# Seeding a PSUM bank with D u, and a planner that dates the parts of a ScalarE block

## The chip, the cores and the metric

The kernel runs on one core of one Trainium2 chip. The metric is the device time of the program in microseconds, median of several runs. All data is float32.

## The reference, cut to what matters

The program is a two-layer network on 8 images of 384 channels x 32 x 32. Layer 0 is a selective state-space block (mamba) in both directions over the 1024 positions plus a gated local convolution. Layer 1 is causal attention with six heads, and a feed-forward part with quantised activations for the first five images. What the change touches:

```python
def step(h, inp):
    dA, dBu, c = inp
    h = dA * h + dBu
    return (h, jnp.einsum('bdn,bn->bd', h, c))
...
y = ys.transpose(1, 0, 2) + u * D_param
y = y * silu(z)
...
h = _bitlinear(x, W1, b1)
h = jax.nn.gelu(h, approximate=False)
out = _bitlinear(h, W2, b2)
```

The states' sum over n, the term D u and the gate silu(z) are the first part of the change. `_bitlinear` scales its result by 128 over the largest magnitude and clips it, and the gelu's input is clipped only where it matters (from above, after the gelu); the second product reads those clips.

## The kernel before

**The scan.** The work of the state-space block is cut into 768 units. A unit is one image, one direction and half of the positions (a "part", four per image), one of three blocks of 128 channels, one of four groups of four states, and one of two halves `q` of the channel block; each unit is a tile g of 128 partitions x 1024. For a unit, GpSimd multiplies delta u by B into g (`s_first`, line 988), ScalarE forms exp(delta A) in a PSUM bank `da`, VectorE scans along the positions, ScalarE copies the last column as a carry in parts that have a successor, and GpSimd multiplies g by C (`s_scan`, line 994). There are six g buffers, and GpSimd's first multiply runs two units ahead. Two units make a pair: TensorE sums the four states of the pair into the single PSUM bank `y` (`s_sum`, line 1020), with the matmul's start flag at the first of four pairs and its stop flag at the last. After eight units the part of that channel block closes (`s_gate`, line 1040): u is loaded from DRAM (one buffer), and VectorE forms D u + y into an SBUF tile `yt` for the direction that comes first. For the second it forms D u + y in the bank, adds `yt`, and multiplies by the gate `z`, and the product goes to DRAM. So 48 closings take one VectorE instruction and 48 take three, and only then may TensorE begin the next sums in the same bank.

**Beside it** run, from lists of steps, the input projections and convolutions of the next images, attention, and the feed-forward part. Its middle (lines 1419 to 1427) is one block of four gelus of 128 x 3072 on ScalarE and a table load, recorded with `together()` so that nothing comes between them, followed by four VectorE clips. The 12 products of each of six groups (line 1432 on) read the four clipped quarters in turn. ScalarE reads each finished group out of its bank. The input gates record a similar block of silus and tanhs.

**The order** is made by a planner. Every instruction is recorded first as an `Op` (line 152); several instructions recorded together are the parts of one `Op`. `record` (line 189) adds up a modelled cost for it and notes in `before` which earlier ops it must follow, by overlapping boxes of the tiles. `place` (line 246) then goes through modelled time: an op becomes ready when the modelled ends of its predecessors are past (plus a signal time of 0.2 when they are on another engine), and each free engine takes the ready op of lowest rank. The rank is the order of recording, less what `hurry` grants: 600 for the scan's slots, 60 for gates, clips and blocks. The resulting order is emitted engine by engine, and each engine's queue then runs in that order on the chip, waiting on semaphores. A block's end in the model is the end of all of its parts, its last table load included.

Of the kernel before, what the change touches and what calls it, by code (L numbers as in the profile page):

```python
# [10 lines left out]
F32 = mybir.dt.float32  # L11
BF16 = mybir.dt.bfloat16
AF = mybir.ActivationFunctionType
ALU = mybir.AluOpType
# [4 lines left out]
P = 128  # L19
# [3 lines left out]
HB = 512  # L23
# [31 lines left out]
V_NORM, V_CW, V_CB, V_DTB, V_D, V_DW, V_DWB, V_BP, V_B2 = 0, 1, 5, 6, 7, 8, 17, 18, 19  # L55
# [3 lines left out]
class View:  # L59


    def __init__(self, tile, ap):
        self.tile, self.ap = tile, ap
# [88 lines left out]
class Op:  # L152
    def __init__(self, name, what, args, kwargs, rank):
        self.name, self.parts, self.rank = name, [(what, args, kwargs)], rank
        self.before, self.behind, self.left = {}, [], 0
        self.tiles = []
        self.ready, self.start, self.end = 0.0, None, None
        self.time = 0.0


class Plan:
# [15 lines left out]
    @contextmanager  # L177
    def together(self):
        self.group = []
        yield  # L180
        self.group = None

    @contextmanager
    def hurry(self, offset):
        self.sooner += offset
        yield
        self.sooner -= offset

    def record(self, name, what, args, kwargs):
        views = [v for v in list(args) + list(kwargs.values()) if isinstance(v, View)]  # L190
        given = kwargs.get("out", args[0] if args else None)
        written = [v for v in (given, kwargs.get("accum_out")) if isinstance(v, View)]
        if self.group:
            op = self.group[0]
            op.parts.append((what, args, kwargs))
        else:
            op = Op(name, what, args, kwargs, len(self.ops) - self.sooner)
            self.ops.append(op)
            if self.group is not None:
                self.group.append(op)  # L200
        cost = self.cost(name, what, args, kwargs, written, views)
        if name == "tensor":
            op.time = max(op.time, cost)
        else:
            op.time += cost
        for v in views:
            t, box = v.tile, v.box()
            write = any(v is w for w in written)
            if not t.users:
                t.order = len(t.kind.queue)  # L210
                t.kind.queue.append(t)
            for other, b in t.writes + (t.reads if write else []):
                if other is not op and not (b[1] < box[0] or box[1] < b[0] or b[3] < box[2] or box[3] < b[2]):
                    op.before[id(other)] = other
            (t.writes if write else t.reads).append((op, box))
            if not t.users or t.users[-1] is not op:
                t.users.append(op)
            if t not in op.tiles:
                op.tiles.append(t)
# [26 lines left out]
    def place(self):  # L246
# [7 lines left out]
        def names(op):  # L254
            return ("scalar", "vector") if op.name == "any" else (op.name,)

        def release(op):
            op.ready = max(
                [b.end + (0.0 if b.name == op.name and not b.dma else self.SIGNAL) for b in op.before.values()],
                default=0.0,  # L260
            )
            for e in names(op):
                heapq.heappush(waiting[e], (op.ready, next(count), op))
                heapq.heappush(events, (op.ready, next(count), e))

        for op in self.ops:
            op.dma = op.parts[0][0] == "dma_start"
            op.left = len(op.before)
            for b in op.before.values():
                b.behind.append(op)  # L270
        users_left = {id(t): len(t.users) for k in self.kinds.values() for t in k.queue}
        for op in self.ops:
            if not op.left:
                release(op)
# [19 lines left out]
        while events:  # L294
# [4 lines left out]
            while moved:  # L299
                moved = False  # L300
                for e in engines:
                    while waiting[e] and waiting[e][0][0] <= now:
                        op = heapq.heappop(waiting[e])[2]
# [5 lines left out]
                    while free_at[e] <= now and ready[e]:  # L309
                        aside, op, held = [], None, set()  # L310
                        while ready[e]:
# [3 lines left out]
                            if fits(item[2], now, held):  # L315
                                op = item[2]
# [7 lines left out]
                        for t in op.tiles:  # L324
                            if t.place is None:
                                k = t.kind
# [10 lines left out]
                        for t in op.tiles:  # L337
                            users_left[id(t)] -= 1
                            if not users_left[id(t)]:
                                at = max(u.end for u in t.users) + self.SIGNAL  # L340
# [10 lines left out]
    def real(self, v, place):  # L351
        if not isinstance(v, View):
            return v
        home = v.tile.kind.places[place]
        return bass.AP(home.tensor, v.ap.offset, v.ap.ap)
# [25 lines left out]
def kernel(  # L381
# [21 lines left out]
    nc = plan = Plan(tc, homes)  # L403
    together, hurry = plan.together, plan.hurry
# [5 lines left out]
    sp = Pool(plan, "scan", 2, bass.MemoryType.SB)  # L410
# [3 lines left out]
    def ctile(name, shape, dt=F32):  # L414
        return const.tile(shape, dt, name=name, tag=name)
# [12 lines left out]
    def bank(name, tag=None):  # L428
        tag = tag if tag in BANKS else "any"
        return ps.tile([P, HB], F32, name=name, tag=tag, bufs=BANKS[tag])  # L430
# [4 lines left out]
    def half(h):  # L435
        return slice(h * HB, (h + 1) * HB)
# [4 lines left out]
    def load(dst, src):  # L441
        nc.sync.dma_start(out=dst, in_=src)
# [8 lines left out]
    spilled = {}  # L451
# [8 lines left out]
    vec = ctile("vec", [P, NC, NV])  # L460
# [8 lines left out]
    for d in range(2):  # L469
        nc.scalar.dma_start(out=wdt[d * DW : d * DW + RANK, :], in_=w_dt)  # L470
        nc.scalar.dma_start(
            out=wdt[d * DW + RANK : d * DW + RANK + 1, :],
# [10 lines left out]
    wproj = ctile("wproj", [P, NC, C])  # L483
    nc.scalar.dma_start(out=wproj, in_=w_proj.rearrange("(c p) e -> p c e", p=P))

    ident = ctile("ident", [P, P])
    make_identity(tc.nc, plan.now(ident))

    cmask = ctile("cmask", [P, HB], BF16)
    nc.vector.memset(cmask, 0.0)  # L490
# [468 lines left out]
    sst = {}  # L959
# [16 lines left out]
    def s_row(u, i):  # L976

        if u.c > 0 or u.q > 0:
            return
        r = sp.tile([P, HB], F32, name=f"bc{i}_{u.name}", tag=f"bc{i}", bufs=NG)  # L980
        rows = spilled[u.b, "rows", u.d][i * NS + u.j * SUB : i * NS + (u.j + 1) * SUB, half(u.h)]
        load(r, rows.partition_broadcast(BLK))
        sst["bc", i, u.b, u.part, u.j] = r
# [36 lines left out]
    def s_sum(u):  # L1020

        if u.q == 0:
            sst["pair"] = sst.pop(("g", u.name))
            return
        if u.j == u.first_group:
            sst["y"] = bank(f"y_{u.name}", "y")
        y = sst["y"]
        pair = (sst.pop("pair"), sst.pop(("g", u.name)))
        with together():
            for k in (2, 3, 0, 1):  # L1030
                nc.tensor.matmul(
                    out=y[k * BLK : (k + 1) * BLK, :],
                    lhsT=gather,
                    rhs=pair[k // 2][:, k % 2, :],
                    start=(u.j == u.first_group),
                    stop=(u.j == u.last_group),
                    skip_group_check=True,
                )

    def s_gate(u):  # L1040

        if not u.closes:
            return
        b, c, h, y = u.b, u.c, u.h, sst["y"]
        key = ("yt", b, c, h)
        t = sp.tile([P, HB], F32, name=f"uh_{u.name}", tag="us", bufs=1)
        load(t, spilled[b, "u", u.d, c][:, half(h)])
        if key not in sst:
            yt = sp.tile([P, HB], F32, name=f"yt_{u.name}", tag="yt", bufs=2 * NC)
            with hurry(offset=60):  # L1050
                nc.vector.scalar_tensor_tensor(
                    yt, t, vec[:, c, V_D : V_D + 1], y, ALU.mult, ALU.add
                )
            sst[key] = yt
            return
        z = sp.tile([P, HB], F32, name=f"zh_{u.name}", tag="z", bufs=1)
        load(z, spilled[b, "z", c][:, half(h)])
        yt = sst.pop(key)
        with hurry(offset=60):
            nc.vector.scalar_tensor_tensor(y, t, vec[:, c, V_D : V_D + 1], y, ALU.mult, ALU.add)  # L1060
            nc.vector.tensor_tensor(y, yt, y, ALU.add)
            nc.vector.tensor_tensor(z, z, y, ALU.mult)
        gy = dram.tile([P, HB], F32, name=f"sgy_{u.name}", tag=f"sp_gy_{c}_{h}")
        nc.sync.dma_start(out=gy, in_=z)
        spilled[b, "gy", c, h] = gy
# [440 lines left out]
    def slots(lo, hi):  # L1506
        def at(f, k):
            if 0 <= k < len(units):
                f(units[k])

        def slot(k):
            at(s_load, k + AHEAD + 2)
            at(lambda u: s_row(u, 0), k + AHEAD + 2)
            at(lambda u: s_row(u, 1), k + 2)
            at(s_first, k + AHEAD)
            at(s_scan, k)
            at(s_sum, k - 1)
            at(s_gate, k - 1)

        def ahead_of_all(k):  # L1520
            with hurry(offset=600):
                slot(k)

        return [(lambda k=k: ahead_of_all(k), 5.0) for k in range(lo, hi)]
# [62 lines left out]
    at = 0.0  # L1587
# [61 lines left out]
```

## Time and profile before

| | |
|---|---|
| median of 3 runs | 4044.43 us (4044.12 to 4044.86) |
| the profiled execution | 4048.24 us |
| its span, first to last instruction | 4046.4 us |
| TensorE clock granted, mean | 0.900 |
| GpSimd's scan multiplies, first start to last end | 74.8 to 3861.3 us |
| VectorE's D u and y steps | 48 x 740, 48 x 747 and 48 x 696 ns |
| gelu block of image 1, first start to last end | 1604.65 to 1615.75 us |

The page gives busy times by engine over the span, the same in 40 slices, and groups of instructions with what ended the idle time before them. Engines are PE (TensorE), DVE (VectorE), ACT (ScalarE), POOL (GpSimd) and SP (SyncE, which issues most DMAs). A matmul of the program in float32 is two instructions in the profile. As all instructions are issued through one recording helper, they bear the same line (L367), so groups are told apart by the names of their tiles: `scan_g` is g, `ps_y` the bank y, `ps_da` the exponentials, `scan_us` the loaded u, `big_big` and `mid_mid` the large tiles of attention and feed-forward.

### The profile page before, as it was taken

The numbers are of one execution on the slowest core, as the hardware profiler recorded it, in microseconds if no ns is written. First come the engines' busy times: TensorE is split into PE (matmuls) and PEld (weight loads), VectorE is DVE, ScalarE is ACT, GpSimd is POOL, SyncE is SP. The second block draws the span as 40 slices with busy tenths as digits, with TensorE's granted clock in tenths as the row PEclk, the third lists the DMA queues.
The fourth block names the chain that finished last, engine by engine and source line by source line (L and its number), as shares of the span: only waits on it lengthen the run. The fifth ranks groups of instructions, "written<-read, shape, count | busy, mean of one in ns | idle before, by whom it ended". The sixth has DMA issues, their size and how long they took to land. (4 is left out here: it accounts for less than half of the span.)

```text
span 4046.4 us, 42961 instructions
## 1 busy us (share of the span) xinstructions
PE 3387.3 (84%) x12426; PEld 1330.0 (33%) x12426; DVE 3264.4 (81%) x4580; ACT 2546.6 (63%) x4967; POOL 3570.8 (88%) x1559
## 2 busy tenths in 40 slices
PE   5585679888699897998986989969989699898899
PEld 1121223333134332343332333323433233333344
DVE  5888987889977899678897687996779977778843
ACT  5666665866746766547667377664676654847635
POOL 2999999999999999789998799987899997999910
PEclk8685779899799898899997999979999799999999
DMA  7547655343563344742445533446334473333300
GB/s 237 194 141 242 235 191 174 100 144 126 202 209 124 102 147 135 247 157 86 134 161 195 183 110 105 138 169 242 123 100 138 142 266 127 113 122 108 128 16 32
DMA packets 338965, 611.99 MB, mean 151 GB/s; under 512 B 34616, under 2 KB 93416, under 8 KB 338728
## 3 DMA queue, kind: packets, MB, share of 16 engines
q1 hardware_dynamic: 329072, 593.10, 43.3%
q10 hardware_dynamic: 9656, 16.15, 1.2%
q8 instruction: 98, 1.61, 0.2%
q14 instruction: 139, 1.14, 0.1%
HBM read 456.03 MB, written 153.09 MB: 151 GB/s over the span
## 5 line engine op out<-in xcount | busy, mean ns | idle before, releaser
L367 POOL TENSOR_TENSOR scan_g<-scan_ud,scan_bc 128x1024 f32<-128x1024 f32 x768 | 1815.9, 2369 | 164.7 <-PE ps_y L367 97.0
L367 POOL TENSOR_TENSOR scan_g<-scan_g,scan_bc 128x1024 f32<-128x1024 f32 x768 | 1816.6, 2369 | 120.9 <-ACT scan_carry L367 66.0
L367 ACT ACTIVATE ps_da<-scan_dl,const_amat 128x512 f32<-128x512 f32 x1536 | 1052.6, 691 | 813.7 <-DVE scan_g L367 800.6
L367 DVE TENSOR_TENSOR_SCAN scan_g<-ps_da,scan_carry,scan_g 128x512 f32<-128x512 f32 x768 | 940.0, 1267 | 111.1 <-POOL scan_g L367 88.0
L367 PE MATMUL ps_any<-big_big,mid_mid 128*128 128x512 f32 x2016 | 952.9, 625 | 78.4 <-DVE big_big L367 56.5
L367 DVE TENSOR_TENSOR_SCAN scan_g<-ps_da,scan_g 128x512 f32<-128x512 f32 x768 | 893.1, 1206 | 127.8 <-POOL scan_g L367 86.9
L367 PE MATMUL ps_y<-scan_g,const_gather 128*32 128x512 f32 x3072 | 467.8, 686 | 275.1 <-POOL scan_g L367 265.0
L367 PEld LDWEIGHTS ps_any<-big_big,mid_mid 128*128 128x128 f32 x2016 | 388.0, 199 | 662.9 <-issue 486.3
L367 PE MATMUL ps_any<-big_big,big_big 128*128 128x512 f32 (+4 forms) x1728 | 551.9, 558 | 15.9 <-DVE small_nm L367 5.3
L367 PE MATMUL ps_any<-const_ident,mid_mid 128*128 128x128 f32 x1728 | 309.4, 304 | 96.0 <-DVE small_nm L367 44.1
L367 DVE CUSTOM_DVE_ANT_0 mid_mid<-ps_any,const_cmask 128x512 f32<-128x512 f32 (+3 forms) x576 | 291.2, 546 | 70.7 <-PE ps_any L367 69.7
L367 PEld LDWEIGHTS ps_any<-big_big,big_big 64*128 64x128 f32 (+1 forms) x1728 | 223.1, 189 | 309.9 <-issue 199.0
L367 DVE SCALAR_TENSOR_TENSOR ps_any<-big_big,const_vec,ps_any 128x496 f32<-128x496 f32 (+6 forms) x420 | 303.1, 727 | 21.6 <-ACT ps_any L367 11.9
L367 PEld LDWEIGHTS ps_any<-const_ident,mid_mid 128*128 128x128 f32 x1728 | 197.9, 149 | 331.2 <-DVE small_nm L367 100.3
L367 ACT COPY ptp_ptn<-ps_any 128x512 f32<-128x512 f32 (+3 forms) x576 | 255.2, 478 | 47.3 <-PE ps_any L367 38.4
L367 PE MATMUL ps_any<-ptp_ptn,big_big 128*64 128x512 f32 (+3 forms) x1152 | 262.3, 536 | 14.6 <-ACT ptp_ptn L367 13.1
L367 ACT ACTIVATE mid_mid<-mid_mid,small_low 128x512 f32<-128x512 f32 (+3 forms) x384 | 242.3, 634 | 47.5 <-DVE small_low L367 47.5
L367 PEld LDWEIGHTS ps_y<-scan_g,const_gather 128*32 128x32 f32 x3072 | 64.2, 114 | 545.0 <-POOL scan_g L367 443.6
L367 PE MATMUL ps_any<-mid_mid,const_onesc 128*128 128x512 f32 x252 | 131.2, 655 | 60.5 <-ACT mid_mid L367 45.6
L367 ACT ACT_TABLE_LOAD x131 | 168.1, 1283 | 2.9 <-PEq L1636 0.7
L367 PE MATMUL ps_any<-mid_mid,const_wdt 25*128 25x512 f32 x192 | 132.1, 852 | 41.6 <-DVE mid_mid L367 32.2
L367 DVE COPY big_big<-ps_any 128x512 f32<-128x512 f32 (+1 forms) x86 | 54.2, 631 | 128.6 <-PE ps_any L367 128.6
(100 smaller groups left out, 3185.4 us busy)
## 6 DMA issues: line engine op xcount, KB each, us to landing
scan_dl<-dram_sp_dl SPq DMA_DIRECT2D x384, 256.0 KB, 3.3
scan_ud<-dram_sp_ud SPq DMA_DIRECT2D x384, 256.0 KB, 3.7
scan_bc<-dram_rows SPq DMA_DIRECT2D x256, 256.0 KB, 3.4
scan_us<-dram_sp_u SPq DMA_DIRECT2D x96, 256.0 KB, 2.7
mid_mid<-dram_sp_u SPq DMA_DIRECT2D x96, 256.0 KB, 4.9
dram_sp_dl<-mid_mid SPq DMA_DIRECT2D x96, 256.0 KB, 4.0
dram_sp_ud<-mid_mid SPq DMA_DIRECT2D x96, 256.0 KB, 4.6
dram_sp_u<-mid_mid SPq DMA_DIRECT2D x42, 512.0 KB, 4.9
```

The costliest lines, as they stand in the source:

```text
L367: getattr(engine, what)(*[mapped(v) for v in args], **{k: mapped(v) for k, v in kwargs.items()})
```

## The change

Part one: the u tile of a part is loaded (`s_skip`, recorded five units before it is used, two buffers), and at the part's opening ScalarE writes D u into the bank `y` (`s_seed`). For the second direction VectorE adds `yt` to it there. All sums then accumulate (`start=False`) on what the bank holds. At the closing the first direction is copied by ScalarE to `yt`, the second is multiplied by `z` by VectorE. One matmul with a start flag at the program's beginning marks the whole bank as written by TensorE.

Part two: an `Op` keeps the modelled end of each of its parts (`upto`), a predecessor is noted together with the last of its parts that matters, and readiness is taken from that part's end (`ends`) and not from the block's.

```diff
@@ class Op
-        self.time = 0.0
+        self.time, self.upto = 0.0, []
+
+    def ends(self, part):
+
+        if self.name == "tensor" or self.dma:
+            return self.end
+        return self.start + self.upto[part]
@@ def record
+        op.upto.append(op.time)
+        part = len(op.parts) - 1
...
-            for other, b in t.writes + (t.reads if write else []):
+            for other, n, b in t.writes + (t.reads if write else []):
...
-                    op.before[id(other)] = other
-            (t.writes if write else t.reads).append((op, box))
+                    op.before[id(other)] = (other, max(n, op.before.get(id(other), (None, 0))[1]))
+            (t.writes if write else t.reads).append((op, part, box))
@@ def place, release
-                [b.end + (0.0 if b.name == op.name and not b.dma else self.SIGNAL) for b in op.before.values()],
+                [
+                    b.ends(n) + (0.0 if b.name == op.name and not b.dma else self.SIGNAL)
+                    for b, n in op.before.values()
+                ],
@@ the beginning
+    nc.tensor.matmul(
+        out=bank("written", "y"),
+        lhsT=ident,
+        rhs=wproj.rearrange("p c e -> p (c e)")[:, :HB],
+        start=True,
+        stop=True,
+    )
@@ def s_sum
-        if u.j == u.first_group:
-            sst["y"] = bank(f"y_{u.name}", "y")
...
-                    start=(u.j == u.first_group),
+                    start=False,
@@ the scan's gates
+    def s_skip(u):
+
+        if not u.opens:
+            return
+        t = sp.tile([P, HB], F32, name=f"uh_{u.name}", tag="us", bufs=2)
+        load(t, spilled[u.b, "u", u.d, u.c][:, half(u.h)])
+        sst["us", u.b, u.c, u.part] = t
+
+    def s_seed(u):
+
+        if not u.opens:
+            return
+        t, y = sst.pop(("us", u.b, u.c, u.part)), bank(f"y_{u.name}", "y")
+        yt, scale = sst.pop(("yt", u.b, u.c, u.h), None), vec[:, u.c, V_D : V_D + 1]
+        with hurry(offset=60):
+            nc.scalar.activation(y, t, AF.Copy, scale=scale)
+            if yt is not None:
+                nc.vector.tensor_tensor(y, yt, y, ALU.add)
+        sst["y"], sst["second"] = y, yt is not None
...
-        t = sp.tile([P, HB], F32, name=f"uh_{u.name}", tag="us", bufs=1)
-        load(t, spilled[b, "u", u.d, c][:, half(h)])
-        if key not in sst:
+        if not sst["second"]:
             yt = sp.tile([P, HB], F32, name=f"yt_{u.name}", tag="yt", bufs=2 * NC)
             with hurry(offset=60):
-                nc.vector.scalar_tensor_tensor(
-                    yt, t, vec[:, c, V_D : V_D + 1], y, ALU.mult, ALU.add
-                )
+                nc.scalar.copy(yt, y)
...
         with hurry(offset=60):
-            nc.vector.scalar_tensor_tensor(y, t, vec[:, c, V_D : V_D + 1], y, ALU.mult, ALU.add)
-            nc.vector.tensor_tensor(y, yt, y, ALU.add)
             nc.vector.tensor_tensor(z, z, y, ALU.mult)
@@ def slot
+            at(s_skip, k + 4)
             at(s_scan, k)
+            at(s_seed, k - 1)
             at(s_sum, k - 1)
             at(s_gate, k - 1)
```

More of the change, by code (lines that the diff above doesn't have):

```diff
@@ L268, in place @@
             op.left = len(op.before)
-            for b in op.before.values():
+            for b, _ in op.before.values():
                 b.behind.append(op)
@@ L1044, in s_gate @@
         b, c, h, y = u.b, u.c, u.h, sst["y"]
-        key = ("yt", b, c, h)
-        t = sp.tile([P, HB], F32, name=f"uh_{u.name}", tag="us", bufs=1)
-        load(t, spilled[b, "u", u.d, c][:, half(h)])
-        if key not in sst:
+        if not sst["second"]:
             yt = sp.tile([P, HB], F32, name=f"yt_{u.name}", tag="yt", bufs=2 * NC)
             with hurry(offset=60):
-                nc.vector.scalar_tensor_tensor(
-                    yt, t, vec[:, c, V_D : V_D + 1], y, ALU.mult, ALU.add
-                )
-            sst[key] = yt
+                nc.scalar.copy(yt, y)
+            sst["yt", b, c, h] = yt
             return
@@ L1057, in s_gate @@
         load(z, spilled[b, "z", c][:, half(h)])
-        yt = sst.pop(key)
         with hurry(offset=60):
-            nc.vector.scalar_tensor_tensor(y, t, vec[:, c, V_D : V_D + 1], y, ALU.mult, ALU.add)
-            nc.vector.tensor_tensor(y, yt, y, ALU.add)
             nc.vector.tensor_tensor(z, z, y, ALU.mult)
```

## The prediction

> **What bounds the kernel now.** I began with the page's busy times and its 40 slices, since the kernel has several stages with different limits.
>
> ```profile
> PE 3387.3 (84%) x12426; PEld 1330.0 (33%) x12426; DVE 3264.4 (81%) x4580; ACT 2546.6 (63%) x4967; POOL 3570.8 (88%) x1559
> POOL 2999999999999999789998799987899997999910
> PEclk8685779899799898899997999979999799999999
> ```
>
> GpSimd (POOL) is the fullest engine and runs at nine tenths nearly everywhere. It holds 1536 scan multiplies that follow each other about every 2.32 us (1536 starts fill the 3562.5 us that their union covers). The dips stand a few slices apart. Windows cut around them show which stages they are:
>
> ```profile
> 1100.00:1600.00 500.00, 492.25 (x214) 0.92 0.46 154
> 1600.00:1860.00 260.00, 218.65 (x95) 0.89 0.51 174
> 1860.00:2130.00 270.00, 267.11 (x116) 0.96 0.39 129
> 2130.00:2400.00 270.00, 222.53 (x97) 0.89 0.50 169
> 2670.00:2900.00 230.00, 184.62 (x80) 0.90 0.53 182
> 3200.00:3420.00 220.00, 178.94 (x78) 0.89 0.56 193
> 3420.00:3862.00 442.00, 439.55 (x190) 0.96 0.34 112
> ```
>
> The columns are window, length, POOL busy, instructions, clock, DMA share, GB/s. In the four stages in which images 1 to 4 go through gelu and the second feed-forward product, POOL idles 41.4 + 47.5 + 45.4 + 41.1 = 175 us. All other time between its start (75 us) and its end (3861 us) has some 45 us of idle. After that come 185 us of the last image's attention, without POOL. The page's chain of waits covers only part of that tail (some 3% of the span), so it does not decide; POOL's own waits do:
>
> ```profile
> POOL scan_g L367 <- PE ps_y L367: 97.0, 24, 12.5
> POOL scan_g L367 <- ACT scan_carry L367: 66.0, 45, 8.1
> POOL scan_g L367 <- DVE scan_g L367: 42.6, 24, 10.9
> ```
>
> (Total us, times, longest.) The first line: the six g buffers are full, because TensorE has not yet summed them. Of its 97.0 us, 22.8 + 24.2 + 28.2 + 18.4 = 93.6 lie in those four stages. The other two lines are ScalarE and VectorE being late with the scan. The timeline of image 1 shows both kinds (start, duration, what, count, idle before it):
>
> ```profile
> 1604.65 11.10 ACT L367 ACTIVATE big_big<-big_big,small_qs 128x3072 f32<-128x3072 f32 x4
> 1615.77 2.57 ACT L367 ACT_TABLE_LOAD   x2
> 1618.35 2.95 ACT L367 ACTIVATE mid_mid<-mid_mid 128x1024 f32<-128x1024 f32 x3
> 1617.46 9.19 DVE L367 TENSOR_SCALAR big_big<-big_big 128x3072 f32<-128x3072 f32 x4
> 1621.69 12.31 PE L367 MATMUL ps_any<-big_big,mid_mid 128*128 128x512 f32 x24 [8.96 <-DVE big_big L367]
> 1629.69 7.14 POOL L367 TENSOR_TENSOR scan_g<-scan_g,scan_bc 128x1024 f32<-128x1024 f32 x3 [9.67 <-DVE scan_g L367]
> 1699.40 20.87 PE L367 MATMUL ps_any<-big_big,mid_mid 128*128 128x512 f32 x48
> 1721.37 4.69 POOL L367 TENSOR_TENSOR scan_g<-scan_ud,scan_bc 128x1024 f32<-128x1024 f32 x2 [7.57 <-PE ps_y L367]
> ```
>
> ScalarE's gelus and the silus right behind them hold it from 1604.65 to 1623.72, 19 us. The clips wait on VectorE for all of the gelus, the products on TensorE for the clips, and POOL starves 9.67 us. Later TensorE pays the delay back: 24 products (48 instructions) in a row, 20.87 us between two sums that POOL's pace would have 9.3 us apart, and POOL stops 7.57 us.
>
> **D u and the gates.** Removed from VectorE: 48 x 740 ns + 48 x 747 ns = 71 us (the groups scan_yt<-scan_us and ps_y<-scan_us). Added to ScalarE: 96 scaled copies into the bank, by the nearest row (ps_any<-big_big,const_vec, 685 ns) 66 us, and 48 copies of y, by ptp_ptn<-ps_any at 128x512 (584 ns), 28 us. ScalarE goes from 2547 to about 2640 us (65%), VectorE from 3264 to about 3193. POOL does none of it, so the sum on the path is nothing by itself. One matmul is added at the start; its weight lands at 10.4 + 12.7 = 23.1 us and TensorE is next wanted at 24.60, so it is nothing.
>
> What frees the y bank changes from one or three VectorE steps (0.74; 0.75 + 0.70 + 0.69 = 2.1 us) to copy and seed (0.58 + 0.69 = 1.3), or product, seed and addition (0.69 + 0.69 + 0.70 = 2.1). So as long as it is not queued, the chain is the same. The next sum is due 9.3 us later, and in the quiet stages POOL is full (492 of 500 us) with today's chain. Queued behind a waiting copy are ScalarE's exponentials of the next units, and VectorE's scans wait for those; today the same wait, 54.7 us in 30 of 96 closings, stands on VectorE, which is the fuller engine. I bound the effect by -5 and +30 us on POOL and take +5, near the row that shows no loss. The u loads (96, 2.7 us) move from the closing to five units before use with a second buffer; SyncE's queue today waits 532 us for the one buffer, yet POOL waits only some 5 us for DMAs after its start, so I count nothing. If that queue blocked the scan loads instead, it would be in those 30.
>
> **Where each engine's work now stands.** The order of instructions of both builds holds no times, but says what TensorE must do between two pairs of sums. I priced a product at 2 x 0.43 us (20.87/48) and let work queue up that exceeds the 8.3 us which POOL's 9.3 us leave beside the sums' own 1.0. The largest backlog of the stages of images 1 to 4:
> before 27.6, 30.0, 30.9, 33.1 us; after 0.6, 24.1, 20.8, 19.0 us.
> Before, POOL lost 93.6 us for 121.6 us of backlog, so about 7 us of each is absorbed by the buffers. With that, after loses 0 + 17 + 14 + 12 = 43 us: a gain of 50 us. The second image gains most: its bursts of 20.6, 18.1, 18.1 and 17.4 us become runs of 7.7.
>
> **The gelus.** Clips stand behind each gelu and no longer behind the block and some 15 convolution steps, and for images 1 to 4 the silu block now stands three or more units behind the gelu block. ScalarE is then held 11.1 + 1.3 us, not 19. The four gaps at the gelus (9.7, 10.9, 7.1, 8.1: 36 us) can shrink by 6.7 each (2.95 + 1.22 of silus and tanhs, two table loads of 1.28), 27 us at most. Two things eat into it. First the clips themselves. This is their record:
>
> ```profile
> 1617.46 4.18 DVE L367 TENSOR_SCALAR big_big<-big_big 128x3072 f32<-128x3072 f32 x1
> ...
> 1621.56 1.75 DVE L367 TENSOR_SCALAR big_big<-big_big 128x3072 f32<-128x3072 f32 x1
> ```
>
> The first one took 4.18 us although it needs 1.75: it ended 1.6 us after POOL's last multiply (1620.02). The Trainium skill, page "SBUF — State Buffer", section "Who interferes with whom", says that such an operation and GpSimd exclude each other for a whole instruction, and that whoever comes first wins. That speaks against this change: clips now fall where POOL still works. By the rule 20 clips x 1.75 = 35 us of POOL may be lost; by the row POOL's next multiply (1617.67) went ahead of a clip already waiting, and the clip ran in POOL's idle time, which costs VectorE and not POOL. I take 8 us, nearer the row. The second: ScalarE's reading of the first finished product stands one or two units behind the gelus, while the product ends some 4 us later; 2 to 3 us in each of four places, 10 us. Net gain 27 - 8 - 10 = 9 us.
>
> **Sum.** -50 - 9 + 5 = -54 us on the profiled execution's span of 4046.4. That execution took 4048.2 us, 3.8 over the median of the runs; I apply the difference to the median: 4044.4 - 54 = 3990 us.
>
> **Rivals.**
> - Everything falls into place: no burst outgrows the buffers (93.6 us) and half of the gelu gaps go (18): -112 us, 3932. For it: POOL is shown full wherever its feeders are smooth. Against it: bursts of 18 to 24 us remain in the new order. With less, down to 3965, 15%.
> - The promised order is not what the chip sees: the clips wait for POOL to starve, so the products start no sooner (TensorE comes out of a stretch at half clock either way), and the bursts wander. Only about 15 us remain: 4030. For it: the lock above. 20%, of which 6% within 0.2% of no change.
> - Slower: seeds and copies on ScalarE. ScalarE takes its work in order; if at each of the 96 part boundaries it waits for TensorE's last sum or VectorE's product with the next exponentials behind it, POOL pays p each time. With p = 1.0 us (of the 1.8 us that VectorE now waits when it waits) that is 96 instead of my 5: 4044 - 59 + 96 = 4081. It is slower than before from p = 0.6 on, and measurably from 0.7. Against it: the quiet stages, where POOL loses next to nothing to such closings on the fuller engine. 15%.
> - My forecast, 50%, 3965 to 4012.
>
> **How the numbers follow.** About 0.2% (8 us) is what a measurement of this kernel can tell from no change. Faster: 50 + 15 + 14 = 79%; same 6%; slower 15%. The range from 3945 to 4050 leaves out the better half of the first rival and most of the slower one.
>
> **What would show it.** In the changed profile POOL's wait for PE ps_y should be about 45 us, near nothing in image 1's stage; runs of TensorE products between sums there some 8 us. The gelu block should end in one table load with exponentials behind it, and POOL's gaps there should be 3 to 7 us. VectorE's busy time should fall by about 71 us, ScalarE's rise by about 90. POOL should stay near full in the stages between. I am wrong if POOL's waits for ACT scan_carry or DVE scan_g grow by as much as the first falls (the boundaries), if clips stretch POOL's multiplies beyond 2.37 us, or if the four stages still hold 170 us of idle.

## The result, and the profile after

The changed kernel takes 4002.52 us (median of 4 runs, 3999.95 to 4005.82), the kernel before in the same session 4044.27 us (4042.36 to 4044.86). The ratio is 0.9898, with a 95% interval of 0.9881 to 0.9915. So 41.8 us were gained, where 54 were forecast, and the time lies inside the range. The profiled execution of the changed kernel took 3999.95 us, its span is 3998.2. That is 48.2 us less than the span before. The difference from 41.8 is where the two profiled executions lie beside their medians, and nothing in the kernel. The sums below are made against the 48.2.

The busy times and the slices of GpSimd and of TensorE's clock, from the page of the changed kernel:

```profile
PE 3389.8 (85%) x12428; PEld 1330.5 (33%) x12428; DVE 3215.7 (80%) x4484; ACT 2629.5 (66%) x5111; POOL 3582.3 (90%) x1559
POOL 3999999999899998999999899988999889999910
PEclk8696879998899997999987999989999889999999
```

VectorE is 49 us less busy, not 71: the 20 clips, whose waiting counts as busy, took 61.4 us in all and not 42.4. ScalarE is 83 us more busy. GpSimd's dips have become shallow. Windows cut around the same stages, as far from each gelu block as those of before (window, length, POOL busy, clock, DMA share, GB/s; the first line is the quiet stretch ahead of image 1's gelu):

```profile
1043.00:1533.00 490.00, 483.18 (x210) 0.93 0.47 159
1533.00:1793.00 260.00, 243.13 (x106) 0.90 0.52 177
2073.00:2343.00 270.00, 246.32 (x105) 0.85 0.49 170
2622.00:2852.00 230.00, 199.80 (x85) 0.90 0.53 185
3150.00:3370.00 220.00, 187.91 (x80) 0.89 0.57 197
```

The four feed-forward stages now hold 16.9 + 23.7 + 30.2 + 32.1 = 103 us of idle, where they held 175. GpSimd's waits show which part went:

```profile
POOL scan_g L378 <- ACT scan_carry L378: 78.6, 32, 10.2
POOL scan_g L378 <- PE ps_y L378: 40.0, 15, 6.8
POOL scan_g L378 <- DVE scan_g L378: 36.8, 24, 4.8
```

The wait for TensorE's sums fell from 97.0 to 40.0 us. The wait behind ScalarE's carry did not fall, it rose from 66.0 to 78.6. The timeline of image 1's gelu says why (start, duration, what, count, idle before it):

```profile
1537.34 11.10 ACT L378 ACTIVATE big_big<-big_big,small_qs 128x3072 f32<-128x3072 f32 x4
1539.41 7.00 POOL L378 TENSOR_TENSOR scan_g<-scan_ud,scan_bc 128x1024 f32<-128x1024 f32 x3
1540.23 7.79 DVE L378 TENSOR_SCALAR big_big<-big_big 128x3072 f32<-128x3072 f32 x1 [0.66 <-ACT big_big L378]
1548.08 9.76 PE L378 MATMUL ps_any<-big_big,mid_mid 128*128 128x512 f32 x18 [11.26 <-DVE big_big L378]
1548.45 1.28 ACT L378 ACT_TABLE_LOAD   x1
1560.97 0.69 ACT L378 ACTIVATE big_big<-ps_any,const_vec 128x512 f32<-128x512 f32 x1 [8.73 <-PE ps_any L378]
1562.84 2.35 POOL L378 TENSOR_TENSOR scan_g<-scan_g,scan_bc 128x1024 f32<-128x1024 f32 x1 [9.53 <-ACT scan_carry L378]
```

The gelus now end in one table load, as planned. The first clip starts 2.9 us after the gelus begin, but it ends at 1548.02, 1.6 us after GpSimd's third multiply (1546.41), and needs 1.75 itself: three multiplies in a row went ahead of it. TensorE's products therefore start at 1548.08. ScalarE's reading of the first finished product, which stands one unit behind the gelus in its queue, then waits 8.73 us with the next exponentials behind it, and GpSimd starves 9.53 us. Image 0 goes the same way:

```profile
1000.66 7.78 DVE L378 TENSOR_SCALAR big_big<-big_big 128x3072 f32<-128x3072 f32 x1
1020.69 0.69 ACT L378 ACTIVATE big_big<-ps_any,const_vec 128x512 f32<-128x512 f32 x1 [8.89 <-PE ps_any L378]
1023.17 2.35 POOL L378 TENSOR_TENSOR scan_g<-scan_g,scan_bc 128x1024 f32<-128x1024 f32 x1 [10.16 <-ACT scan_carry L378]
```

In images 2 to 4 the reading stands one and a half or two units behind the gelus, and does not wait at all. In image 2 the clips came first, and GpSimd paid in another way:

```profile
2089.82 1.73 DVE L378 TENSOR_SCALAR big_big<-big_big 128x3072 f32<-128x3072 f32 x1
2090.05 3.72 POOL L378 TENSOR_TENSOR scan_g<-scan_g,scan_bc 128x1024 f32<-128x1024 f32 x1 [0.64 <-DVE scan_g L378]
```

A multiply that takes 2.35 us alone took 3.72, since a clip of 1.73 had begun 0.23 us before it.

**One account for all kernels.** A span is the time up to GpSimd's first multiply, the union of its multiplies, its idle time between them, and the tail after the last. I divide the idle time by the place where a gap ends: in the 40 us after the start of one of the five gelu blocks ("gelu"), from 40 to 240 us after it ("products"), and everywhere else ("quiet"). This is added up from the starts and ends in each trace, in us:

| kernel | start | gelu | products | quiet | union | tail | span |
|---|---|---|---|---|---|---|---|
| before | 74.8 | 51.7 | 131.5 | 40.9 | 3562.5 | 185.2 | 4046.4 |
| changed | 72.7 | 40.0 | 80.0 | 45.1 | 3574.0 | 186.4 | 3998.2 |
| e1 seeds only | 77.0 | 42.3 | 89.3 | 31.2 | 3566.4 | 183.6 | 3989.8 |
| e2 planner only | 72.3 | 51.8 | 86.3 | 61.9 | 3573.2 | 185.2 | 4030.7 |
| e3 gelu block by its end | 75.2 | 48.1 | 62.0 | 41.3 | 3566.2 | 185.2 | 3977.8 |
| e4 other form of clip | 73.5 | 59.4 | 77.0 | 41.1 | 3559.8 | 185.0 | 3995.8 |
| e5 model alone | 74.8 | 51.5 | 99.0 | 67.5 | 3565.5 | 176.1 | 4034.4 |
| e6 gelu alone | 75.2 | 47.2 | 116.6 | 32.9 | 3575.5 | 183.5 | 4030.9 |
| e7 clip dated longer | 73.8 | 39.8 | 99.9 | 39.4 | 3573.4 | 185.2 | 4011.6 |
| e8 gates later | 74.1 | 39.1 | 59.8 | 44.1 | 3572.9 | 186.5 | 3976.5 |
| e9 early u | 76.6 | 48.1 | 110.5 | 48.3 | 3566.5 | 185.2 | 4035.2 |
| e10 seeds on VectorE | 74.9 | 54.0 | 118.4 | 126.4 | 3575.4 | 180.2 | 4129.1 |
| e11 other form, dated | 74.5 | 41.3 | 97.1 | 43.4 | 3560.1 | 185.2 | 4001.6 |
| e12 nudged | 73.5 | 49.5 | 91.3 | 46.7 | 3567.2 | 183.6 | 4011.7 |

### The profile page after: what moved, and what is told of

The parts are those of the page before. It is cut to its first block, busy times and chain, and to the rows that moved or that the text cites. A ratio compares the mean times of both kernels' runs of the same rounds, so it can differ in the third digit from the quotient of the medians.

```text
span 3998.2 us, 43071 instructions
## 1 busy us (share of the span) xinstructions
PE 3389.8 (85%) x12428; PEld 1330.5 (33%) x12428; DVE 3215.7 (80%) x4484; ACT 2629.5 (66%) x5111; POOL 3582.3 (90%) x1559
## 5 line engine op out<-in xcount | busy, mean ns | idle before, releaser
L378 POOL TENSOR_TENSOR scan_g<-scan_g,scan_bc 128x1024 f32<-128x1024 f32 x768 | 1828.2, 2383 | 121.5 <-ACT scan_carry L378 78.6
L378 POOL TENSOR_TENSOR scan_g<-scan_ud,scan_bc 128x1024 f32<-128x1024 f32 x768 | 1838.9, 2398 | 103.1 <-DMA scan_ud<-dram_sp_ud 59.5
L378 PE MATMUL ps_any<-ptp_ptn,big_big 128*64 128x512 f32 (+3 forms) x1152 | 267.2, 544 | 13.4 <-ACT ptp_ptn L378 12.4
L378 ACT ACTIVATE mid_mid<-mid_mid,small_low 128x512 f32<-128x512 f32 (+3 forms) x384 | 242.5, 634 | 42.3 <-DVE small_low L378 42.0
L378 PE MATMUL ps_any<-mid_mid,const_onesc 128*128 128x512 f32 x252 | 130.2, 652 | 42.3 <-ACT mid_mid L378 30.9
L378 ACT COPY mid_mid<-ps_any 128x512 f32<-128x512 f32 x234 | 130.9, 582 | 43.0 <-PE ps_any L378 36.4
```

The source lines that it names most:

```text
L378: getattr(engine, what)(*[mapped(v) for v in args], **{k: mapped(v) for k, v in kwargs.items()})
```

## The experiments

My theory after the result: the gain is the shorter bursts of products, and dating the gelus by their parts gives back what it saves. Rivals: one of the two parts of the change does it all; or the order is chance.

**e1, the seeds alone, and e2, the planner alone.** Each keeps one part of the diff above and the other side as it was before.

> Only the first part of the change (D u seeded into the bank); the planner dates blocks by their end as before. The order of its instructions already differs: largest TensorE backlog between sums in the stages of images 1 to 4 7.7, 29.6, 24.8 and 27.6 us (before 27.6, 30.0, 30.9, 33.1). Theory (TensorE's bursts decide): POOL's wait for PE ps_y falls from 97 to about 62 us, and two of four silu blocks leave the gelus: 4005 to 4020 us. Rival (dating the parts is all of the gain, seeds are neutral): 4040 to 4048 us. Rival (ScalarE's closings cost POOL at each boundary): over 4052 us.

> Only the second part (parts of blocks dated); the gates stay as before. Backlogs in its order 2.0, 26.9, 27.4, 23.9 us. Theory (bursts decide, either part can smooth them): POOL waits about 57 us for PE ps_y, total 4002 to 4015 us. Rival (the gain is the 71 us that leave VectorE): 4035 to 4048 us.

The seeds alone took 3992.6 us (ratio 0.9872, 0.9858 to 0.9885), less than the whole change and 12 us under the range of its theory. The planner alone took 4032.9 us (0.9972, 0.9962 to 0.9983), near the range of its rival and 18 us above that of its theory. Both shorten the bursts: the idle time under the products falls by 42 and by 45 us. The planner alone pays it back, with 21 us more in the quiet stages and 11 us of stretched multiplies; the seeds alone lose nothing there, their quiet stages improve by 10.

**e3, the change with the gelu block dated by its end.** Every other block is still dated by its parts.

```diff
     def ends(self, part):
...
+        if any(k.get("func", None) == AF.Gelu or AF.Gelu in args for _, args, k in self.parts):
+            return self.end
```

> The whole change, but the gelu block alone is dated by its end as before, so clips and products stand late again, while silus, tanhs and softplus are dated part by part. Backlogs in its order 0.7, 22.4, 24.8, 20.2 us, about those of the change; silus stand right behind the gelus again for images 2 to 4. Theory (bursts decide, and early clips collide with POOL's multiplies, which eats what the gelus gain): within 10 us of the changed kernel, 3993 to 4012 us. Rival (early clips and products are the gain): 4025 to 4044 us.

It took 3977.2 us (0.9835, 0.9821 to 0.9848): 25 us better than the changed kernel and 16 us under the range of its theory. The profiled spans differ by 20 us. Of these, the changed kernel saves 8 us of gaps at the gelus, loses 8 us to stretched multiplies, 18 us more under the products, and 4 us in the quiet stages.

**e4, the clips in another form, in the changed kernel's order.** The clip is min, then an addition of 0 with an accumulator; the values are the same.

```diff
...
-    nc.vector.tensor_scalar(st["h", q], st["h", q], QCLIP, None, ALU.min)
+    nc.vector.tensor_scalar(
+        st["h", q], st["h", q], QCLIP, 0.0, ALU.min, ALU.add, accum_out=sink
+    )
```

> The changed kernel with the clip in the form that also gives a sum (min, then adding 0), in exactly the same order. The page on SBUF says this form does not take GpSimd's port. Theory (the clip and POOL's multiplies exclude each other): clips last about 3.3 us each but never stretch a multiply, which stays at 2.32 to 2.37 us, the first clip is never held 7.8 us, the 10 us gaps for ACT scan_carry at images 0 and 1 shrink to under 4; 3978 to 3992 us. Rival (the exclusion is a side show): 3998 to 4008 us. If the longer clips delay products as much as the lock did: 4000 to 4010 us too, with the gaps kept but no stretched multiply.

It took 3998.4 us (0.9888, 0.9872 to 0.9903), in the range of the first rival and not of the theory. The clips by form (min/median/max ns, first and last start), first of the changed kernel, then of e4:

```profile
L378 DVE TENSOR_SCALAR big_big<-big_big x20: 1731/2634/7790, 1000.7 to 3176.2; 128x3072 f32<-128x3072 f32 x20
```

```profile
L378 DVE TENSOR_SCALAR_CACHE_REDUCE big_big<-big_big x20: 3325/3346/3353, 998.0 to 3177.0; 128x3072 f32<-128x3072 f32 x20
```

In this form a clip takes 3.3 us always, and no multiply beside it is stretched: the union falls by 14 us. But four such clips take 13.4 us. In image 1 the last of them ends 19.5 us after the gelus begin (20.7 in the changed kernel), ScalarE's reading of the first product still waits, 7.59 us there, and the gaps at the gelus grow by 19 us in all. So the lock is real, and 14 us of GpSimd's time go with it; but it is not the whole cost of early clips.

**e5, another order and nothing else.** The kernel before, whose planner counts VectorE's D u + y steps at 0.01 us (`light` is set around these steps alone).

```diff
+        if what == "scalar_tensor_tensor" and self.light:
+            return 0.01
...
```

> The kernel before, computing exactly what it did, but its planner is told that VectorE's D u + y steps cost 0.01 us each. So only the order of the instructions changes. The seeds alone gave -52 us; this asks whether that came from less work on the chip or from another order. Largest backlogs of TensorE by order, images 1 to 4: 12.4, 30.0, 26.6, 23.6 (before 27.6, 30.0, 30.9, 33.1). Theory that the order decides: less 7 each, 65 us of lost POOL time against 94, so -29, and one more gelu without silus right behind, -4: about 4012. Theory that VectorE's 71 us of real work and its queue decide: nothing changes on the chip but luck, 4036 to 4052, or slower, since the plan is now untrue.

It took 4037.9 us (0.9981, 0.9974 to 0.9989). Under the products it gained 32.5 us, where the backlogs of its order said 29. It gave back 26.6 in the quiet stages, and 9.1 of the 12 us by which its span is shorter lie in its tail. GpSimd's waits:

```profile
POOL scan_g L370 <- ACT scan_carry L370: 87.4, 53, 10.2
POOL scan_g L370 <- DVE scan_g L370: 62.6, 46, 10.9
POOL scan_g L370 <- PE ps_y L370: 52.3, 15, 9.6
```

The last line has fallen by 45 us against the kernel before, the first two have risen by 21 and 20. In the plan the 96 steps of D u cost VectorE nothing; on the chip they still took 0.75 us each.

**e6, the seeds and only the gelu block dated by its parts.** The condition of e3, turned round.

> The seeds, and in the planner the gelu block alone is dated by its parts; all other ScalarE blocks by their end. Against the seeds alone (3992.6) this adds just the early clips and products. Backlogs 14.9, 28.7, 29.4, 32.2 (seeds alone 7.7, 29.6, 24.8, 27.6): +15 us. Theory that dating the gelus is harmful in itself (ScalarE's reading of the first product stands 1 to 1.5 units behind the gelus, before the product can be there): another +11, as from the seeds alone to the changed kernel at the gelus, so about 4018. Rival, that early clips help and something else in the changed kernel costs: 3985 or less at the gelus, 4000 with the backlogs.

It took 4033.5 us (0.9971, 0.9959 to 0.9983), 41 us more than the seeds alone. I expected 25. At the gelus it lost 5, and the union grew by 9 (some 7 of it are multiplies stretched at the gelus), about as in the theory. Under the products it lost 27, where the difference of the backlogs said 15. That difference is one of two counts: against the kernel before, e6's own count is -16 and its measured change -15, while the seeds alone did 10 better than their count of -32. In two of its images the first clip took 9 and 11.3 us.

**e7, the changed kernel with a clip counted at 3.0 us, not 1.83.**

```diff
-            return 0.05 + n * 0.00058
+            return 3.0 if n == NC * L else 0.05 + n * 0.00058
```

> The changed kernel, whose planner is told 3.0 us for a clip of 128 x 3072 and not 1.83. ScalarE's reading of the first product then stands 2 to 2.5 units behind the gelus, not 1 to 2; all else of the change stays. Theory that this reading, too early in ScalarE's queue, makes the gaps of 14 us in images 0 and 1: they fall to 6 to 8, with backlogs about level (3.7, 28.2, 18.6, 18.1 against 0.6, 24.1, 20.8, 19.0), so -13 us: about 3990. Rival, that the clips' lock with GpSimd makes them: the clips stand where they stood, so 3998 to 4006.

It took 4013.8 us (0.9926, 0.9914 to 0.9939): a miss. In images 0 and 1, ScalarE's reading stands later. Its own waits fell from 8.9 and 8.7 us to 2.9 and 2.5, and the gaps from 14.0 and 13.6 us to 10.6 and 9.4, not to 6 to 8; the first clip still took 7.8 and 7.0 us. In image 2 the lock now fell the other way: the first clip took 10.4 us, and the gap went from 2.7 to 13.3. Under the products it lost 20. So the place of the reading matters, but it does not outweigh the rest.

**e8, the kernel of e3 with the gates' blocks of silus moved back by rank.** No gelu block has silus right behind it.

```diff
-                with hurry(offset=60), together():
+                with hurry(offset=-300), together():
```

> As the version with the gelu block dated by its end (3977), but the blocks of silus and tanhs of the input gates are recorded with a rank 360 later, so that none of them stands right behind a gelu block (with one table load and one unit between, in all five images; there it was three images with both stacked). Theory that stacking costs ScalarE some 7 us and POOL about 5 to 6 in each of those three: -17 us, less +7 for image 4's backlog (27.6 against 20.2): about 3967. Rival, that POOL's gap at a gelu comes from the clips and products and not from the stacking: 3977 to 3985.

It took 3977.5 us (0.9833, 0.982 to 0.9846), the same as e3: a miss. The gaps at the gelus fell by 9 us, half of what I expected. But the clips then fell where GpSimd was working, and its union grew by 6.7. What ScalarE no longer withheld, the lock took.

**e9, only the u loads made early.** The loads of the seeds, with the kernel before's steps on VectorE.

```diff
-        t = sp.tile([P, HB], F32, name=f"uh_{u.name}", tag="us", bufs=1)
-        load(t, spilled[b, "u", u.d, c][:, half(h)])
+        t = sst.pop(("us", b, c, u.part))
...
+            at(s_skip, k + 4)
```

> The kernel before with one part of the seeds alone: the u tiles are loaded five units before use, with two buffers. D u, y and the gates stay on VectorE as before. Backlogs of TensorE by order, images 1 to 4: 12.4, 30.0, 30.9, 33.1 (before 27.6, 30.0, 30.9, 33.1), and image 1's gelu has no silus right behind it. Theory that the seeds gained because VectorE was relieved: as when the model alone was changed, the shorter burst is paid back by later scans, 4035 to 4046. Theory that backlogs alone decide: -15 and -4, 4025. Theory that the load was what held the closings: below 4015; VectorE's waits of before show none for it.

It took 4035.9 us (0.9976, 0.9967 to 0.9985). Its order gained 21 us under the products (15 by the backlogs), 7 went back in the quiet stages. So the early load alone does not bring the seeds' gain.

**e10, the seeds written by VectorE.**

```diff
-            nc.scalar.activation(y, t, AF.Copy, scale=scale)
-            if yt is not None:
-                nc.vector.tensor_tensor(y, yt, y, ALU.add)
+            if yt is None:
+                nc.vector.tensor_scalar(y, t, scale, None, ALU.mult)
+            else:
+                nc.vector.scalar_tensor_tensor(y, t, scale, yt, ALU.mult, ALU.add)
```

> The seeds alone with the old planner, but VectorE writes D u into the bank (in the second direction D u + yt in one instruction) and ScalarE only copies y. VectorE is then relieved of 34 us of 71, and ScalarE gets 28 us more, not 94. Backlogs 18.5, 29.1, 30.9, 32.2 (seeds alone 7.7, 29.6, 24.8, 27.6; before 27.6, 30.0, 30.9, 33.1). Theory that the relief of VectorE lets the order's gain come through: about half of the 52 us, 4010 to 4025. Theory that the early seed, on whatever engine, is what counts: as the seeds alone, 3990 to 4000 (with its backlogs +17, up to 4010). Theory that only ScalarE's taking it over counts: 4035 or more.

It took 4130.9 us (1.0214, 1.02 to 1.0228), far outside everything expected, and it does not tell those theories apart, since it did not relieve VectorE at all: that engine was busy for 3376 us, 112 more than before. Its step for the second direction, by form, and one closing in the timeline:

```profile
L367 DVE SCALAR_TENSOR_TENSOR ps_y<-scan_us,const_vec,scan_yt x48: 752/2490/10278, 322.9 to 3915.0; 128x512 f32<-128x512 f32 x48
```

```profile
877.16 6.20 DVE L367 SCALAR_TENSOR_TENSOR ps_y<-scan_us,const_vec,scan_yt 128x512 f32<-128x512 f32 x1
878.13 2.37 POOL L367 TENSOR_TENSOR scan_g<-scan_g,scan_bc 128x1024 f32<-128x1024 f32 x1
880.43 2.38 POOL L367 TENSOR_TENSOR scan_g<-scan_ud,scan_bc 128x1024 f32<-128x1024 f32 x1
884.52 0.69 ACT L367 ACTIVATE ps_da<-scan_dl,const_amat 128x512 f32<-128x512 f32 x1 [10.10 <-DVE scan_g L367]
885.96 2.35 POOL L367 TENSOR_TENSOR scan_g<-scan_g,scan_bc 128x1024 f32<-128x1024 f32 x1 [3.15 <-ACT scan_carry L367]
```

The instruction takes 0.75 us when nothing is in its way, and a median of 2.49. Here it ended at 883.36, half a microsecond after GpSimd's second multiply; the scans came behind it, and GpSimd stood still for 3.15 us. The 48 of them took 184 us in all, 148 more than 48 x 0.75. The quiet stages hold 85 us more of idle time than before. The seeds' addition in e1, with one operand in SBUF and one in the bank, took 671 to 697 ns each time.

**e11, e4's clips with the planner told their 3.3 us.**

> The changed kernel with clips in the form that also accumulates (min, then add 0: the same values), which showed no lock with GpSimd and 3.3 us, and with the planner told 3.3 us for it, so that ScalarE's reading of the first product stands 2 to 2.5 units behind the gelus. Theory that the clips' lock and the early reading together make what dating the gelus costs: gaps at the gelus of some 8 us in each image and no stretched multiplies; against the version that was told 3.0 us with locking clips (4013.8) 10 to 15 less, so about 4000, its backlogs (3.4, 28.2, 18.6, 18.1) being the same. Rival, that early products cost something else (TensorE's products pushed in front of the sums): gaps as before and 4010 to 4020.

It took 4001.9 us (0.989, 0.9876 to 0.9903), as expected. The gaps at the gelus are 6.3, 8.4, 8.7, 9.6 and 8.3 us, no longer 2.6 to 13.3 as in e7, and the union is 13 us shorter. So without the lock and with the reading in its later place the kernel is 12 us better than e7. It is still 25 us behind e3, by the 35 us more under the products.

**e12, the changed kernel with a signal counted at 0.21 us, not 0.20.**

> The changed kernel, whose planner takes 0.21 us and not 0.20 for a signal between engines: nothing of the change is altered, but the order comes out a little different everywhere. It shows how much of a difference of some us between two builds is chance of the order. Backlogs 0.3, 28.2, 21.1, 18.5 (changed kernel 0.6, 24.1, 20.8, 19.0): +4; which of clip and multiply comes first at each gelu is open, 5 to 10 us either way. 3995 to 4018; outside of that, chance is larger than I think and single comparisons of 15 us prove little.

It took 4010.4 us (0.9915, 0.9901 to 0.9928), 8 us more than the changed kernel. So the chance of the order is worth some 8 us here (one pair only): of the differences above, e7's 11 and e11's 12 us and the 10 us between the seeds alone and the changed kernel lie near it, e4's 4 us within it. At a single gelu it is worth more: image 1's gap fell from 13.6 to 3.5 us, image 2's rose from 2.7 to 8.9. The five kernels that date all blocks by their parts with ScalarE's seeds (changed, e4, e7, e11, e12) took 3998 to 4014 us, the two that date the gelus by their end (e3, e8) 3977. That difference, 21 us at the least, is larger than what this one pair shows.

## Why the prediction was right, point by point

**The bound.** It held: each span of the table is GpSimd's union, its idle time and its two ends. Of the 48.2 us between before and changed, 51.5 are idle time under the products; the rest of the account nearly cancels.

**The bursts.** Forecast -50 us, measured -51.5 (131.5 to 80.0 under the products). The wait for PE ps_y was to be about 43 to 45 and was 40.0, near nothing in image 1 (all its idle time under the products is 3.2 us), and the longest runs of products there between two sums take 7.99 us. Counting the backlog in the order of instructions, with some 7 us of each absorbed, told GpSimd's wait for TensorE's sums. Under the products that wait was 87.9 us before. In eleven of the twelve kernels whose four backlogs are on record, it fell by what the count says to within 7 us: by 51 us in the changed kernel (count 50), 53 in e3 (47), 35 in e5 (29), 13 in e6 (16), 46 in e7 (50), 17 in e9 (15). In e10 it fell by 24 (count 11). What the count does not tell is the waits behind ScalarE's carry and VectorE's scans in the same stages. They were 34 us before and 39 in the changed kernel, so here the count was also the change in idle time. In e3 they are 23, and in e7 and e11 they are 48 and 47; there the idle time missed the count by 22, 18 and 15 us.

**D u and the gates.** Forecast +5, measured +4.2 in the quiet stages, but the agreement is luck. The 40 us ahead of the five gelus hold 7.8 us more of idle time than before (18.2 against 10.4), and all other quiet time 3.6 us less. The 7.8 us do not come from the seeds: with the seeds alone those stretches hold 10.8 us, with the planner alone 20.8. So the seeds cost GpSimd nothing that can be seen here, and the ScalarE waits that the slower rival feared are there without effect. Also, the step's reason was incomplete. It said "POOL does none of it, so the sum on the path is nothing by itself". In e2, e5 and e9 the orders with shorter bursts lose 21, 27 and 7 us in the quiet stages, all on a VectorE that still does the D u steps. With them gone (e1, e3) those stages change by -10 and +0.4. This fits that the 71 us of VectorE's work are worth something: without them the bursts' gain stands. But it is not shown apart from the earlier place of D u in the bank, since e10, which was to separate the two, did not. Booked by cause and not by place, most of the gain belongs to the seeds (-52 alone, -30 on top of the planner), not to the planner (-12 alone), which the prediction's terms don't show; each of these kernels also has another order.

**The gelus.** Forecast -9, measured -0.2: gaps -11.7, union +11.5. This is the term that was mis-sized, by 9 us, more than the whole miss of 5.8 us in span. By image, the gaps went from 6.2, 11.0, 12.7, 11.3 and 10.4 us to 14.0, 13.6, 2.7, 3.5 and 6.2. For images 1 to 4, of which alone the prediction speaks, that is -19.4, where 27 - 10 = 17 were forecast. Image 0 was put at nothing without a reason, and it lost 7.8: before, its gaps held only 6.2 us, and now it has the same held clip and early reading as image 1. The stretched multiplies, put at 8 us, took the 11.5: 11 of them last 2.8 to 3.9 us, and one did before.

The step that failed was "POOL's next multiply (1617.67) went ahead of a clip already waiting, and the clip ran in POOL's idle time, which costs VectorE and not POOL": what waits for a clip was left out of it. In images 0 and 1 of the changed kernel three multiplies went ahead, the clip took 7.8 us, and the products waited with it; the reading of the first product stood one unit behind the gelus and waited 8.9 and 8.7 us, not the 2 to 3 us allowed for. In images 2 to 4 no clip took longer than 3.3 us, and ten multiplies were stretched.

Beside e3 the term is worse than nothing. Dating the gelus costs 20 us of span, 18 of them under the products. There, waits for ScalarE's carry rose from 11.6 to 21.0 us and those for VectorE's scans from 11.8 to 17.7. In the three kernels with ScalarE's seeds that date the gelus by their end (e1, e3, e8) the two waits together are 21 to 29 us, in the six that date them by their parts 35 to 48. That the blocks of silus were moved out from behind the gelus is not enough to explain it: e8 moves them out in images 2 to 4 too, by one unit, and its idle time under the products is 59.8 us where e3 has 62.0. Whether it is the products out of step with the sums, or where the silus came to stand instead, stays open.

**The rivals.** The best case, 3932, had bursts of 18 to 24 us against it, and they are there (25 us of idle on average under the products of images 2 to 4). That the order does not reach the chip is refuted for the bursts and true for the clips. The slower case needed 0.6 us at each of 96 boundaries; ScalarE does wait there (41.7 us for VectorE's product, 18.2 for the last sum), but GpSimd's waits for ScalarE's carry in the quiet stages, without the 40 us ahead of the gelus, are 9.7 us as they were before, where 58 us more were needed.

**The signs.** Of the three signs of being wrong, one came: multiplies stretched beyond 2.37 us, to 3.9. The waits for ScalarE's carry grew by 13 us where the first line fell by 57, and the four stages hold 103 us and not 170. The gaps at the gelus were to be 3 to 7 us; the longest in images 0 to 4 are 10.2, 9.5, 1.7, 3.1 and 5.7.

**Better than both.** The change without the gelu block's part ends, e3, takes 3977 us: 1.65% less than before, where the change takes 1.02% less.

## What to carry to other kernels

Read a planner's new order as backlogs: how much work stands between two things that the bottleneck waits for, in the pace it needs. That gave the bottleneck's wait for TensorE to within 7 us in nearly every build here. It says nothing of the waits for the other engines, and these decided whether the gain stayed. Before a long instruction is brought forward, ask what may overtake it and what in another engine's queue stands ready to wait for its result: an instruction earlier in the plan and not earlier on the chip turns into a wait with everything else behind it.

## What the runs showed that was not expected

- A 128 x 3072 clip of 1.75 us can be held for 7.8 us, in e6 11.3, by GpSimd multiplies that follow each other, since the next multiply is ahead of the waiting clip each time. When the clip is first, the multiply stretches from 2.35 us to as much as 3.9. With an accumulator, the clip takes 3.3 us each of 40 times and neither happens.
- A reading that stands too early in its engine's queue stops what is behind it. In the fourteen kernels, ScalarE's reading of the first product stands one unit behind the gelus in six places, and it waits there 3.9 to 9.6 us. In the other 64 it waits 5.1 us at most.
- A VectorE instruction on two operands in SBUF, with its output in a PSUM bank, took 0.75 to 10.28 us beside GpSimd's multiplies. The Trainium skill, page "SBUF — State Buffer", section "Who interferes with whom", says that an instruction with two SBUF inputs contends with a GpSimd instruction that reads SBUF; the trace agrees, and the kernel that has 48 of them is the only one here that is slower than before, by 86 us.
- A bank that TensorE has once written whole with a start flag keeps accumulating on what ScalarE and VectorE write into it later: all sums of the changed kernel run without a start flag, in 96 parts.
